# One DVE cost counted as 1.9 instead of 1.2, and a reordered start and last step, in a kernel bound by TensorE

## Chip, cores and metric

One core of one Trainium2 chip. The metric is the device time of the kernel in microseconds (us). Engines are named as in the profile: PE (TensorE matmuls), DVE (VectorE), ACT (ScalarE), POOL (GpSimd), SP (SyncE, which here only issues DMAs). "L685" is line 685 of the kernel in question; the same statement has different line numbers before and after the change, so the text says each time which statement is meant.

## The reference, cut to what matters

```python
# x: [32, 512, 512] float32; adj: 512 x 512 of 0 and 1, about 0.8% ones
h = relu(layernorm(x))                                   # layer 0
q, k, v = h @ Wq, h @ Wk, h @ Wv                         # 8 heads of 64
attn = softmax(q k^T / 8 + (1 - adj) * -1e9)
x = x + (attn v) @ Wo + bo

h = relu(layernorm(x))                                   # layer 1
hw = h @ W
e = leaky_relu(s1[i] + s2[j]) * adj                      # s1 = hw @ a1, s2 = hw @ a2
x = x + elu(softmax(e) @ hw + beta * hw)
```

## The kernel before

The kernel walks over the 32 graphs in overlapping steps: step b computes the attention of graph b while it does Wo for graph b-1 and layer 1 for graph b-2. Each of the 512x512x512 products with a weight (Q, K, V, Wo, and W of layer 1) is done as 7 products of 256-blocks instead of 8; such a product is 7 "pieces" of 1.73 us on PE, with additions on DVE and POOL around them. A head pair is a "unit" (four in a step, numbered 0 to 3, so the third is j == 2, called unit 2): 4 groups of scores, exponentials on ACT, sums of them on DVE (`total`), the product with the values, and a division (`finish`: a reciprocal on DVE, a DMA round trip that spreads it, a multiply on POOL).

In the traces of the kernel before, DVE runs its instructions in the order in which the program issues them: the lines of all 4207, in the order of their starts, are those of the built program. Where a DVE instruction goes is decided by a reckoned clock, when the program is built:

```python
def pe(us):                                   # called after each piece of PE work
    clock["pe"] += us
    till = clock["pe"] + (1.0 if at_ends[0] else 0.4)
    while True:
        ...
        fits = [(by, i) for i, (_, t, cost, _, by) in enumerate(spare)
                if max(clock["dve"], t) + cost <= till]
        ...
            run_spare(min(fits)[1])           # earliest "by" first
        ...                                   # nothing fits: go on with PE

def later(key, wait, by, cost, fn):           # puts an item into the list of spare DVE work
    now = max(clock["dve"], clock["pe"])
    spare.append((key, now + wait, cost, fn, now + by))
```

So the cost given to `later` is not a statement about the chip. It is a number that decides what stands in front of what in DVE's queue.

```python
# scores: the sums of exponentials of unit j (k = 1, 2, 3)
later("es", 2.2 if k < T - 1 and b > 1 else 1.2, gap(b, j) - 6.0 + k, 1.2, lambda: total(k, e))

# finish: the division
def divide():
    nc.vector.reciprocal(rq, pd)                       # 1.75 us
    then("rd", spread)                                 # DMA round trip, then a multiply on POOL
later("rd", 0.0, gap(b, (j + 1) % NP) - 4.0, 1.7, divide)

# out_proj: what empties the banks of the Wo product
def add(i, k, p):
    for r, p_ in parts(k, i, p):
        nc.vector.scalar_tensor_tensor(r, p_, 1.0 / VS, r, op0=ALU.mult, op1=ALU.add)
def more(q_):                                          # shares of the second piece, on POOL
    for i in (1, 0):
        for r, q in parts(1, i, q_):
            nc.gpsimd.tensor_tensor(r, r, q, op=ALU.add)

# diagonal of layer 1: row sums by matmul, then the diagonal blocks
product(nc, pd[:, t, :], mixed(st["as"])[:, t, :], ones[:, :HD], ...)
for k in range(T):
    nc.vector.scalar_tensor_tensor(d, ident, bd[:, k : k + 1], d, op0=ALU.mult, op1=ALU.add)

# row_constants: 16 dots of W with a, once, in the start
later("wa", 8.0, 60.0, 0.5, lambda g=g, c=c, o=o, ar=ar: dot(g, c, o, ar))

# order of the parts of a step; digits are units, "." their denominators
order = {
    0: "0.V1.NH2c.3wK.Q", 1: "0.VUrR1.W2.NH3K.Q", B - 1: "0.VDU1.rRGX2.W3.t", B: "0yrR.zUWDngY",
    B + 1: "DgJY",
}.get(b, "0.VDU1.rgY2.RMNH3.KQ")     # V, K, Q: products; M, W: Wo; D: diagonal; g, G: gather; Y: product with W
```

## Time and profile before

| | before |
|---|---|
| time, median of 3 (lowest, highest) | 3651.6 us (3647.19, 3654.03) |
| profiled span | 3650.6 us |
| PE idle in the whole span | 124 us |
| of these between 200 and 3490 us (steps 2 to 30) | 66.6 us |
| mean granted PE clock | 0.992 |

PE is busy for 97% of the span and nothing else comes near. Such a profile is read from its gaps: which gap comes back in every step, who ended it, and what stood in front of that releaser in its own queue. The lines are in the prediction below. In a list of waits, "PE qz_w L53 <- DVE x L685: 42.7, 28, 2.6" means: before writing the bank qz_w, PE stood idle 42.7 us in all, 28 times, at most 2.6 us, and the last thing that it waited for was the DVE instruction of line 685. In a timeline a line is start, duration, engine, line, operation, and in brackets the idle time before it and who ended that.

### The profile page before, as it was taken

The numbers are of one execution on the slowest core, as the hardware profiler recorded it, in microseconds if no ns is written. First come the engines' busy times: TensorE is split into PE (matmuls) and PEld (weight loads), VectorE is DVE, ScalarE is ACT, GpSimd is POOL, SyncE is SP. The second block draws the span as 40 slices with busy tenths as digits, with TensorE's granted clock in tenths as the row PEclk, the third lists the DMA queues.
The fourth block names the chain that finished last, engine by engine and source line by source line (L and its number), as shares of the span: only waits on it lengthen the run. The fifth ranks groups of instructions, "written<-read, shape, count | busy, mean of one in ns | idle before, by whom it ended". The sixth has DMA issues, their size and how long they took to land. (4 is left out here: it accounts for less than half of the span.)

```text
span 3650.6 us, 64127 instructions
## 1 busy us (share of the span) xinstructions
PE 3526.5 (97%) x26358; PEld 1884.4 (52%) x26358; DVE 2757.1 (76%) x4207; ACT 1459.3 (40%) x2310; POOL 1320.0 (36%) x1090
## 2 busy tenths in 40 slices
PE   9899999999999999999999999999999999999986
PEld 5455554555555555545555555555455555455543
DVE  6778777778777787777787777877777877777774
ACT  3344434334443444343344434443434444343432
POOL 5333343333333333433333333334333333423341
PEclk9999999999999999999999999999999999999997
DMA  4011111101111011111011110111110111111110
GB/s 134 18 33 44 47 47 44 36 27 47 47 47 36 30 45 47 47 44 36 27 47 47 47 38 28 44 47 47 44 36 27 47 47 47 47 32 31 41 38 27
DMA packets 109548, 155.02 MB, mean 42 GB/s; under 512 B 16513, under 2 KB 54913, under 8 KB 109249
## 3 DMA queue, kind: packets, MB, share of 16 engines
q1 hardware_dynamic: 106640, 148.49, 12.9%
q8 instruction: 209, 3.42, 0.4%
q10 hardware_dynamic: 2400, 2.10, 0.2%
q14 instruction: 91, 0.74, 0.1%
q0 software_dynamic: 208, 0.27, 0.0%
HBM read 116.66 MB, written 34.15 MB: 41 GB/s over the span
## 5 line engine op out<-in xcount | busy, mean ns | idle before, releaser
L585 ACT ACTIVATE e<-e 128x1024 f32<-128x1024 f32 x512 | 541.3, 1057 | 263.4 <-DVE e L570 227.3
L570 DVE SCALAR_TENSOR_TENSOR e<-maskT,ps 128x1024 f32<-128x1024 uint8 x384 | 455.7, 1214 | 115.6 <-PE ps L558 115.3
L558 PE MATMUL ps<-qT,kT 64*128 64x512 f32 x2048 | 490.0, 608 | 27.5 <-DVE dmax L798 18.1
L645 POOL TENSOR_TENSOR oT<-oT,rd 128x512 f32<-128x512 f32 x128 | 167.6, 1310 | 864.1 <-DMA rd<-rd 710.6
L608 PE MATMUL po<-e,v 128*64 128x512 f32 x2048 | 463.2, 594 | 0.0
L53 PE MATMUL pg<-at,hn 128*64 128x512 f32 x2048 | 451.6, 599 | 4.2 <-DVE dmax L798 2.1
L558 PEld LDWEIGHTS ps<-qT,kT 64*128 64x128 f32 x2048 | 184.4, 186 | 329.8 <-issue 155.2
L582 DVE TENSOR_TENSOR es<-es,e 128x1024 f32<-128x1024 f32 x254 | 342.3, 1348 | 15.2 <-ACT e L585 0.7
L501 POOL TENSOR_TENSOR qT<-qT,edge 128x256 f32<-128x256 f32 x128 | 85.4, 689 | 658.9 <-DVE qT L497 658.8
L53 PEld LDWEIGHTS pg<-at,hn 128*64 128x64 f32 x2048 | 146.4, 138 | 293.9 <-issue 284.7
L359 DVE TENSOR_SCALAR x<-x,mv,rs 128x512 f32<-128x512 f32 x128 | 104.5, 858 | 226.9 <-POOL rs L334 226.7
L608 PEld LDWEIGHTS po<-e,v 128*64 128x64 f32 x2048 | 141.9, 137 | 235.5 <-issue 223.6
L834 POOL TENSOR_TENSOR y<-y,x 128x512 f32<-128x512 f32 x124 | 159.2, 1288 | 191.2 <-DVE y L826 188.1
L635 DVE RECIPROCAL rd<-pd 128x256 f32<-128x256 f32 x128 | 223.9, 1749 | 3.1 <-POOL oT L645 3.1
L664 POOL TENSOR_TENSOR x<-x,c_row 128x512 f32<-128x512 f32 x124 | 165.2, 1352 | 100.8 <-DMA x<-in_x_dram 100.8
L766 ACT ACTIVATE at<-at 128x512 f32<-128x512 f32 x128 | 80.7, 630 | 278.2 <-DVE at L762 277.0
L53 PE MATMUL qz_y<-w,vT 128*64 128x256 f32 x1520 | 181.3, 381 | 4.1 <-DVE yq L847 4.1
L582 DVE TENSOR_TENSOR es<-e,e 128x1024 f32<-128x1024 f32 x127 | 172.4, 1357 | 0.8 <-PE pd L626 0.8
L824 DVE TENSOR_SCALAR y<-y 128x512 f32<-128x512 f32 x128 | 55.3, 432 | 155.5 <-ACT y L821 155.1
L812 ACT COPY gT<-pg 128x512 f32<-128x512 f32 x128 | 74.9, 585 | 243.9 <-PE pg L53 243.9
L53 PE MATMUL qz_w<-wo,uT 128*64 128x256 f32 x1040 | 127.6, 388 | 46.3 <-DVE x L685 42.7
L739 DVE CUSTOM_DVE_ANT_0 scr<-hn,wa_r 128x512 f32<-128x512 f32 x256 | 163.6, 700 | 0.1
(223 smaller groups left out, 6395.6 us busy)
## 6 DMA issues: line engine op xcount, KB each, us to landing
x<-in_x_dram SPq DMA_DIRECT2D x128, 256.0 KB, 4.0
rd<-rd SPq DMA_DIRECT2D x256, 128.0 KB, 2.9
out_dram<-y SPq DMA_DIRECT2D x128, 256.0 KB, 4.0
x<-in_x_dram SPq DMA_DIRECT2D x63, 512.0 KB
s<-row_s SPq DMA_DIRECT2D x32, 256.0 KB, 3.8
rd<-rd ACTq DMA_DIRECT2D x128, 4.0 KB
adj<-in_adj_dram SPq DMA_DIRECT2D x4, 256.0 KB, 6.4
wk<-in_L_gnn_Wk_dram ACTq DMA_DIRECT2D x3, 256.0 KB
```

Of the source, the lines that this page charges most:

```text
L53: nc.tensor.matmul(out[s : s + HD], lhsT[:, s : s + HD], rhs, start=start, stop=stop, skip_group_check=onto)
L359: nc.vector.tensor_scalar(xs[t], xs[t], mv[:, t, 0:1], rstd[:, t : t + 1], op0=ALU.subtract, op1=ALU.mult)
L558: nc.tensor.matmul(ps[s], st["kT"][j][rows, ts(k, P)], st["qT"][j][rows, :], start=True, stop=True)
L570: nc.vector.scalar_tensor_tensor(e, maskT[:, k, :].unsqueeze(1).to_broadcast([P, 2, N]), NEG, p, op0=ALU.mult, op1=ALU.add)
L582: (nc.gpsimd if early else nc.vector).tensor_tensor(es, one, e, op=ALU.add)
L585: nc.scalar.activation(e, e, AF.Exp)
L608: nc.tensor.matmul(po[s * HD : (s + 1) * HD, :], v[k // 2][:, k % 2, (2 * j + s) * HD : (2 * j + s + 1) * HD], e[k][:, s, :], start=k == 0 ...
L635: nc.vector.reciprocal(rq, pd)
L645: then("rd", lambda: nc.gpsimd.tensor_tensor(o, o, rd, op=ALU.mult), 6.0)
L664: eng.tensor_tensor(r[:, t, :], r[:, t, :], c_row, op=ALU.add)
L739: nc.vector.tensor_tensor_reduce(scr, st["hn"][t], r, 1.0, 0.0, op0=ALU.mult, op1=ALU.add, accum_out=st["s12"][:, g, t : t + 1],)
L834: (nc.vector if b == B - 2 else nc.gpsimd).tensor_tensor(yu, yu, x_[:, :, ts(i, H)], op=ALU.add)
```

## The change

It is meant to rearrange the last step (logits sooner, diagonals inside the Wo product and inside the final product, no DMA trip in the last division), to move the 16 dots of the start, and, in every step from 2 on, to count the sums of exponentials of the third unit (j == 2) as 1.9 us instead of 1.2. Cut to its core:

```diff
-                    later("wa", 8.0, 60.0, 0.5, ...dot...)
+                    later("wa", 40.0, 75.0, 0.5, ...dot...)
...
-                    "es", 2.2 if k < T - 1 and b > 1 else 1.2, gap(b, j) - 6.0 + k, 1.2, lambda: total(k, e)
+                    "es", 2.2 if k < T - 1 and b > 1 else 1.2, gap(b, j) - 6.0 + k, 1.9 if j == 2 and b > 1 else 1.2,
+                    lambda: total(k, e)
...
+        if (b, j) == (B - 1, NP - 1):
+            return finish_last(b, j, st)
...
-        later("rd", 0.0, gap(b, (j + 1) % NP) - 4.0, 1.7, divide)
+        later("rd", 0.0, gap(b, (j + 1) % NP) - 4.0 if (b, j) != (0, NP - 1) else 0.0, 1.7, divide)
+    def finish_last(b, j, st):      # 2 matmuls spread the denominators; no DMA
...
+        def divide(k):
+            nc.vector.reciprocal(pd[:, ts(k, H)], pd[:, ts(k, H)])
+            if k:
+                nc.vector.tensor_tensor(o, o, pd, op=ALU.mult)
...
-        eng = nc.vector if b == B - 1 else nc.gpsimd         # residual rows
-                eng.tensor_tensor(r[:, t, :], r[:, t, :], c_row, op=ALU.add)
+                nc.gpsimd.tensor_tensor(r[:, t, :], r[:, t, :], c_row, op=ALU.add)
...
-            for i in (1, 0):
+            def share(i):
                 for r, q in parts(1, i, q_):
                     nc.gpsimd.tensor_tensor(r, r, q, op=ALU.add)
+            share(1)
+            st["share"] = lambda: share(0)
...
             fourth(b - 1, "uT", prev["oT"])      # combination t4, on POOL
+            prev["share"]()                       # second share now behind it
             run(pieces)
...
-            0: "0.V1.NH2c.3wK.Q", 1: "0.VUrR1.W2.NH3K.Q", B - 1: "0.VDU1.rRGX2.W3.t", B: "0yrR.zUWDngY",
-            B + 1: "DgJY",
+            0: "0.V1.NH2c.3wK.Q", 1: "0.VUrR1.W2.NH3K.Q", B - 1: "0.VDU1.rRGX2.W3.ft",
+            B: "0p.qmURzviDlngPES", B + 1: "gJY",
```

Cut away: the helpers behind the new letters. Of those, "i" is six of the seven Wo pieces, with step 30's totals forced in; "l" is the last piece, behind the diagonal; "P", "E" and "S" are the same for the final product.

More of the change, by code (lines that the diff above doesn't have):

```diff
@@ L323, in row_constants @@
                 for o in range(2):
-                    later("wa", 8.0, 60.0, 0.5, lambda g=g, c=c, o=o, ar=ar: dot(g, c, o, ar))
+                    later("wa", 40.0, 75.0, 0.5, lambda g=g, c=c, o=o, ar=ar: dot(g, c, o, ar))
     def stats(src, name, mv):
@@ L648, in finish @@
         release()
-        later("rd", 0.0, gap(b, (j + 1) % NP) - 4.0, 1.7, divide)
+        later("rd", 0.0, gap(b, (j + 1) % NP) - 4.0 if (b, j) != (0, NP - 1) else 0.0, 1.7, divide)
+    def finish_last(b, j, st):
+        pd = psum.tile([P, N], F32, name=f"pd_{b}_{j}", tag="pd")
+        for s in range(2):
+            nc.tensor.matmul(
+                pd[s * HD : (s + 1) * HD, :], ones[:, :HD], st["es"][j][:, s, :], start=True, stop=True
+            )
+        pe(0.95)
+        o = st["o"][j // 2][:, j % 2, :]
+        def divide(k):
+            nc.vector.reciprocal(pd[:, ts(k, H)], pd[:, ts(k, H)])
+            if k:
+                nc.vector.tensor_tensor(o, o, pd, op=ALU.mult)
+        finished.add((b, j))
+        st["largest"] = lambda: nc.scalar.activation(
+            pd, pd, AF.Copy, accum_out=rsum[:, b, j : j + 1]
+        )
+        for k in range(2):
+            later("rd", 0.0, 0.0, 1.7 + 0.7 * k, lambda k=k: divide(k))
     def residual(b, st, i, tag="x1", bufs=3):
@@ L894, in G, with first_y, more_y @@
                 gather(b - 2, c, old)
+        def first_y(g):
+            states[g]["pieces"] = final(g, states[g])
+            next(states[g]["pieces"])
         def y_(g):
+            first_y(g)
+            more_y(g)
+        def more_y(g):
             st = states[g]
-            st["pieces"] = final(g, st)
-            for _ in range(3):
+            for _ in range(2):
                 next(st["pieces"])
@@ L911, in Y, with most_of_y @@
             z_(b - 2)
+        def most_of_y():
+            y_(b - 2)
+            run_all(("at", b - 1))
+            for _ in range(3):
+                next(old["pieces"])
         def X():
@@ L928, in W, with most_of_w @@
         def W():
+            most_of_w()
+            run(prev["pieces"])
+        def most_of_w():
             need("wa")
             fourth(b - 1, "uT", prev["oT"])
-            run(out_proj(b - 1, prev))
+            prev["pieces"] = out_proj(b - 1, prev)
+            for k in range(6):
+                next(prev["pieces"])
+                if k == 1:
+                    prev["share"]()
+                elif k == 2 and b == B:
+                    run_all(("at", b - 2))
         def H_():
@@ L952, in M @@
             fourth(b - 1, "uT", prev["oT"])
+            prev["share"]()
             run(pieces)
@@ L960, in step @@
             "y": lambda: y_(b - 3), "z": lambda: z_(b - 3), "X": X, "M": M, "g": G1,
-            "K": K, "U": U, "H": H_, "r": lambda: residual(b - 1, prev, 0, *(("e", 4) if b == B else ())),
+            "K": K, "U": U, "H": H_, "r": lambda: residual(b - 1, prev, 0),
             "t": T1, "n": lambda: run_all(("hn", b - 1)), "J": judge,
@@ L964, in step @@
             "Q": lambda: run(proj_q(b + 1, nxt)),
+            "p": lambda: first_y(b - 3), "q": lambda: more_y(b - 3), "v": lambda: prev["largest"](),
+            "m": lambda: run_all(("hn", b - 2)),
+            "i": most_of_w, "l": lambda: run(prev["pieces"]),
+            "P": most_of_y, "E": lambda: diagonal(b - 1, prev), "S": lambda: z_(b - 2),
+            "f": lambda: residual(b, cur, 0, "x", 4),
             "c": lambda: value_row(ao, bvr), "w": row_constants,
```

## The prediction

> **What bounds the kernel now.** I read the page first, then who waited for whom on PE, then PE's timeline over the whole span with its gaps, and last the timelines of DVE and POOL around the gaps that come back.
>
> ```profile
> span 3650.6 us, 64127 instructions
> PE 3526.5 (97%) x26358; PEld 1884.4 (52%) x26358; DVE 2757.1 (76%) x4207; ACT 1459.3 (40%) x2310; POOL 1320.0 (36%) x1090
> ```
>
> PE is the bound: 97% busy, DVE next with 76%. Nothing in the change takes matmuls away, so all it can win is the 124 us (3650.6 - 3526.5) in which PE stands still, and the time in which PE runs at a lower granted clock because it stood still. So the question is where those 124 us are:
>
> ```profile
> PE qz_w L53 <- DVE x L685: 42.7, 28, 2.6
> PE pe L53 <- DVE as L773: 20.4, 2, 13.0
> PE ps L558 <- DVE dmax L798: 18.1, 24, 1.3
> ...
> PE qz_w L53 <- POOL uT L399: 2.4, 2, 1.3
> ```
>
> Columns: total us, times, longest. Two of these come back every step (28 and 24 times in 32 steps of about 111.4 us), one sits in the last two steps (twice, up to 13 us). The first is the last piece of the Wo product. One step of it, PE and then DVE:
>
> ```profile
> 1739.54 1.95 PE L53 MATMUL qz_w<-wo,uT 128*64 128x256 f32 x16 [1.17 <-DVE x L685]
> ...
> 1735.26 1.74 DVE L635 RECIPROCAL rd<-pd 128x256 f32<-128x256 f32 x1
> 1736.92 0.62 DVE L685 SCALAR_TENSOR_TENSOR x<-x_w,x 128x512 f32<-128x512 f32 x1
> 1737.47 1.32 DVE L582 TENSOR_TENSOR es<-es,e 128x1024 f32<-128x1024 f32 x1
> 1738.71 0.68 DVE L685 SCALAR_TENSOR_TENSOR x<-qz_w,x 128x512 f32<-128x512 f32 x1
> ```
>
> PE may not write that bank again before the second L685 has read it, and ahead of that L685 in DVE's queue stand a reciprocal (1.74) and the last sum of exponentials (1.32) of unit 2. The second recurring wait is behind the diagonal; PE, DVE, POOL:
>
> ```profile
> 2135.74 3.27 PE L558 MATMUL ps<-qT,kT 64*128 64x512 f32 x12 [0.70 <-DVE dmax L798]
> ...
> 2130.84 4.62 DVE L792 SCALAR_TENSOR_TENSOR at<-ident,bd,at 128x128 f32<-128x128 f32 x4
> ...
> 2131.15 1.28 POOL L645 TENSOR_TENSOR oT<-oT,rd 128x512 f32<-128x512 f32 x1 [20.44 <-DMA rd<-rd]
> ...
> 3564.53 1.51 DVE L792 SCALAR_TENSOR_TENSOR at<-ident,bd,at 128x128 f32<-128x128 f32 x4
> ```
>
> The four small L792 take 4.62 us beside POOL's multiply and the three combinations after it, and 1.51 us where POOL is idle (last line, in the tail). The start and the tail:
>
> ```profile
> 128.69 2.08 PE L558 MATMUL ps<-qT,kT 64*128 64x512 f32 x4 [3.64 <-DVE e L570]
> ...
> 157.99 2.91 PE L53 MATMUL qz_w<-wo,oT 128*64 128x256 f32 x16 [2.80 <-POOL oT L379]
> ...
> 3563.00 1.23 PE L53 MATMUL pe<-ones,as 128*64 128x64 f32 x16 [7.41 <-DVE as L773]
> ...
> 3608.76 1.23 PE L53 MATMUL pe<-ones,as 128*64 128x64 f32 x16 [12.96 <-DVE as L773]
> ...
> 3612.07 16.14 PE L53 MATMUL pg<-at,hn 128*64 128x512 f32 x64 [2.08 <-DVE dmax L800]
> ```
>
> A gather (x64) takes 13.95 us in the middle of the kernel and 16.14 us here: PE runs at the low clock for a while after the long wait.
>
> [...] the mean granted clock is 0.51 in 7 us around the 3.64 us wait at 128 us, and 0.66 in the 5 us from the end of two of the three waits of 2.5 us (622 and 1626 us; 1.00 at 959); it stays 1.00 after the waits of 1.5. [...] 4.62 against 1.51 us above; L582 takes 1.2 us alone and 2.1 beside POOL. [...]
>
> **The change part by part.**
>
> *1. Third unit's sums counted as 1.9 instead of 1.2.* No instruction is added. The kernel keeps a reckoned clock for PE and DVE, and puts a spare DVE item into the queue when (DVE clock + cost) is within 0.4 of the PE clock. I followed that rule by hand through a middle step; with 1.2 it gives DVE's order in the trace. Zero is the start of unit 2's scores. PE's clock after Wo pieces 1 to 7 is 5.76, 7.49, 9.22, 10.95, 12.68, 14.41, 16.14.
> Before: piece 2 takes two normalisations (6.95), piece 3 sums 1 and 2 (9.35), piece 4 the reciprocal (9.35 + 1.7 = 11.05, limit 11.35), then L685, then piece 5 sum 3 (11.8 + 1.2 = 13.0, limit 13.08): the order that costs the wait.
> After: piece 3 has room only for sum 1 (8.85), piece 4 for sum 2 (10.75); in piece 5 neither the reciprocal (11.7 + 1.7 = 13.4) nor sum 3 (13.6) fits under 13.08, nor in piece 6. They go behind piece 7. L685 then runs as soon as piece 5 is done, about 1.7 us before PE needs its bank. That removes the waits of steps 2 to 30: 42.7 - 0.8 (step 1) + 2.4 (the combination t4, which now also goes before the second share on POOL, 1.3 to 1.7 us sooner) = **-44 us**, and two spells of low clock after waits of 2.54 (groups of 3.06 and 3.54 us instead of 1.95): **-3**.
>
> *2. Its consequence at the diagonal.* By the same rule the backlog of about 3 us moves the dots, the logits and the totals later through K, Q and V; the last total then stands right before the diagonal, and the reciprocal of unit 3, so far in the fourth piece of V, goes behind it. So POOL's multiply, which follows it by a DMA round trip (5.2 us from reciprocal's end to L645), no longer lies beside L792: 1.5 instead of 4 to 5 us, and scores need not wait. What that wait costs is more than its 0.70: from 2133.90 to the next group at 2138.93 are 5.03 us, without the wait 3.64, so 1.4; 24 such and 5 of about 0.7 (2245 us) make 37. The order is delicate, so I count **-30**. Against it: the last total ends by my count 12.05 us after V's start and the diagonal wants it at 12.13; a semaphore's latency of 0.1 to 0.2 gives **+3** over the 28 steps.
>
> *3. Start.* The 16 dots (L309) become ready at +40 instead of +8, so the five us of them at 122.4 to 127.4, directly ahead of the scores' L570, go away: 3.64 of wait and 3.0 of low clock (2.08 + 1.08 + 3.52 against 1.07 + 0.64 + 1.95). The reciprocal of (0,3), now due at once, ran at 144.8 and can run near 130; POOL's combinations, which PE waited 2.80 + 1.7 of low clock for, come some 14 us sooner. Sum 11; other spare items take the place of the dots, so **-10**.
>
> *4. Tail, from 3514 on.* The last division loses its DMA trip: two reciprocals of 1.75 on DVE and a multiply (about 0.7) instead of one reciprocal and 128 KB twice. Added for PE: two matmuls, 0.9. Residual rows move from DVE (3.57 us) to POOL. Laid out by the trace's durations: the denominator must wait for the former one's copy (3522.7): PE loses 3. The dots of step 30, 1.6 us each beside POOL and ended at 3547.4, end near 3533, so its logits are done about 3550 behind the elu's. The diagonal goes into Wo before its last piece, the gather starts at about 3554.5 instead of 3566.3 and keeps the full clock: end 3568.5 against 3583.0, **14** won. Step 31's logits: statistics from 3555, dots to 3564, row back at 3569.5 (before 3578.9); its totals by 3577.5 beside the last product of step 30. Three elu's of DVE (9.1 us as at 3591 to 3600) stand before the diagonal's own 2 us, so the last gather starts at about 3588.5 instead of 3612.1: 23 won; the rest (38.5 us) stays. I take **-21**.
>
> Sum: -10 - 44 - 3 - 30 + 3 - 21 = -105; 3651.6 - 105 = about **3547 us**.
>
> **Rivals.** (a) *Only the Wo wait goes.* The totals come too late at the diagonal, or the reciprocal does not move as reckoned, so that a wait on L773 takes the place of that on L798. For it: the margin of 0.1 us. Then -75, 3577, at the edge of 2%. (b) *DVE's backlog turns into new waits in K, Q or unit 3*, because 0.7 x 3 us is reckoned each step and other items come in front of evictions. For: DVE stands at 76%, 77 in the middle. Against: real items are shorter than their reckoned cost (dots 0.62 against 0.8, logits 1.39 against 1.5). With 1 us per step it makes 3580 to 3590. (c) *The tail gains nothing*: the long waits there are on chains (dots, row through DRAM, exponentials), and reordering moves the wait; then 3565. (d) All of parts 1 and 2, and no new wait: 3535.
>
> **Range and chances.** Part 1 is nearly sure (44 of 47), parts 3 and 4 are 31 give or take 10, part 2 is 0 to 37. The range reaches from all of it (3525) to part 2 missing with a weaker tail (3582). Two per cent is 73 us, 3578.6: 86% faster, 13% within, 1% slower.
>
> **What will show it.** Right, if the list of PE's waits has no more L685 line in the middle, if L792 in the middle takes 1.5 us for four and L798 is gone, if steps are 108.5 to 109 us long, if nothing waits at 128 us, and if the last gather starts about 24 us nearer to the end of step 31's scores. Wrong, if L773 or es shows as PE's releaser some 28 times, or if PE's waits on kT, qT or e appear in K, Q or unit 3.

## The result, and the profile after

| | median us | lowest to highest | runs |
|---|---|---|---|
| before | 3652.82 | 3647.19 to 3656.22 | 4 |
| after | 3560.49 | 3559.8 to 3561.33 | 4 |

The ratio is 0.9749, 95% interval 0.9732 to 0.9766: 2.5% faster. Here and below a ratio is the mean time of one kernel's runs over that of the other's of the same rounds, so it is not quite the ratio of the medians quoted. The page of the kernel after:

```profile
span 3559.0 us, 64141 instructions
PE 3506.1 (99%) x26353; PEld 1885.4 (53%) x26354; DVE 2727.3 (77%) x4207; ACT 1452.9 (41%) x2310; POOL 1396.6 (39%) x1095
```

PE does the same work in 20 us less busy time and is idle 53 us instead of 124. Busy time falls in part because PE runs less at the low clock (mean granted clock 0.994 instead of 0.992), and in part because a group of matmuls that a wait splits takes longer: in the prediction's example 5.03 us instead of 3.64 for a listed wait of 0.70, at a granted clock of 1.00. Who waits on PE now, after:

```profile
PE ps L558 <- DVE e L570: 11.6, 6, 8.5
PE qz_w L53 <- DVE y L853: 5.8, 1, 5.8
PE pg L53 <- DVE dmax L827: 5.5, 1, 5.5
```

The two lines that came back 28 and 24 times are gone, and so are both waits on the totals (`as`). What is left are single waits in the start and the tail. Between 200 and 3400 us PE is busy for 3198.4 of 3200 us.

**Where the 92 us come from.** I cut the two timelines at the same piece of work, the first piece of a Wo product, in step 2 and in step 31. Before, then after:

```profile
277.57 1.95 PE L53 MATMUL x_w<-wo,oT 128*64 128x256 f32 x16
...
3494.47 1.95 PE L53 MATMUL x_w<-wo,oT 128*64 128x256 f32 x16
```

```profile
280.08 1.95 PE L53 MATMUL x_w<-wo,oT 128*64 128x256 f32 x16
...
3412.79 1.95 PE L53 MATMUL x_w<-wo,oT 128*64 128x256 f32 x16
```

| stretch | before | after | difference | predicted |
|---|---|---|---|---|
| start, to the Wo product of step 2 | 277.6 | 280.1 | +2.5 | -10 |
| middle, 29 steps | 3216.9 (110.93 each) | 3132.7 (108.03 each) | -84.2 | -74 (-44 - 3 - 30 + 3) |
| tail, from the Wo product of step 31 | 156.1 | 146.2 | -9.9 | -21 |
| sum | 3650.6 | 3559.0 | -91.6 | -105 |

So over nine tenths of the gain is in the middle, where the only changes are the cost of 1.9 and the place of one share on POOL. The rearranged last step, which is most of the diff, gives a tenth.

**The Wo product in the middle, after** (DVE, then PE; compare the step at 1739 us in the prediction):

```profile
1696.70 0.68 DVE L709 SCALAR_TENSOR_TENSOR x<-x_w,x 128x512 f32<-128x512 f32 x1
1698.11 0.69 DVE L709 SCALAR_TENSOR_TENSOR x<-qz_w,x 128x512 f32<-128x512 f32 x1 [0.73 <-POOL uT L399]
...
1702.00 1.75 DVE L638 RECIPROCAL rd<-pd 128x256 f32<-128x256 f32 x1
...
1699.45 1.90 PE L53 MATMUL qz_w<-wo,uT 128*64 128x256 f32 x16
```

L709 is the former L685. The one that frees the bank qz_w ends at 1698.80; PE comes for it at 1699.45 and has no bracket, so no wait. The reciprocal, and after it the third sum, now stand behind it.

**The diagonal in the middle, after** (DVE):

```profile
1648.15 1.55 DVE L819 SCALAR_TENSOR_TENSOR at<-ident,bd,at 128x128 f32<-128x128 f32 x4
...
1650.00 1.76 DVE L638 RECIPROCAL rd<-pd 128x256 f32<-128x256 f32 x1
```

The four small instructions take 1.55 us instead of 4.62, as the reciprocal comes behind them and POOL's multiply, which hangs on it, starts only at 1657.09. All 128 of them, single durations (shortest, median, longest, in ns), before and after:

```profile
L792 DVE SCALAR_TENSOR_TENSOR at<-ident,bd,at x128: 436/1457/1657, 235.8 to 3611.3; 128x128 f32<-128x128 f32 x128
```

```profile
L819 DVE SCALAR_TENSOR_TENSOR at<-ident,bd,at x128: 437/455/1628, 237.6 to 3520.3; 128x128 f32<-128x128 f32 x128
```

**The start, after.** PE, DVE and POOL:

```profile
152.50 2.08 PE L558 MATMUL ps<-qT,kT 64*128 64x512 f32 x4 [8.48 <-DVE e L570]
165.11 2.83 PE L53 MATMUL qz_w<-wo,uT 128*64 128x256 f32 x16 [2.35 <-ACT qz_w L464]
...
136.74 0.42 DVE L309 CUSTOM_DVE_ANT_0 scr<-w,a 128x256 f32<-128x256 f32 x1
137.08 1.49 DVE L309 CUSTOM_DVE_ANT_0 scr<-a_w,a 128x256 f32<-128x256 f32 x1
...
151.24 1.21 DVE L570 SCALAR_TENSOR_TENSOR e<-maskT,ps 128x1024 f32<-128x1024 uint8 x1
...
139.67 5.68 POOL L688 TENSOR_TENSOR x<-x,c_row 128x512 f32<-128x512 f32 x4
```

The waits of 3.64 at 128 us and of 2.80 at 158 us are gone, as predicted. In their place stands one of 8.48 us: the dots (L309) did not go away but stand before a later L570, and most of them take 1.47 to 1.49 us instead of 0.42. The first, at 136.74, still takes 0.42: POOL was between two instructions, of which one ended at 136.80 and the next started at 136.88. From 135.53 to 151.03 POOL is busy, with no break over 0.1 us.

**The tail, after** (DVE, then POOL):

```profile
3447.19 1.22 DVE L748 SCALAR_TENSOR_TENSOR nb<-mv,rs 128x2 f32<-128x2 f32 x1 [3.71 <-POOL rs L334]
...
3459.32 2.79 DVE L853 SCALAR_TENSOR_TENSOR y<-yq,rd,y 128x256 f32<-128x256 f32 x2
...
3467.16 1.64 DVE L789 SCALAR_TENSOR_TENSOR at<-at 128x512 f32<-128x512 f32 x1
...
3445.21 1.27 POOL L648 TENSOR_TENSOR oT<-oT,rd 128x512 f32<-128x512 f32 x1 [12.73 <-DMA rd<-rd]
3446.45 0.71 POOL L334 TENSOR_TENSOR rs<-rs,mhalf 128x2 f32<-128x2 f32 x1
```

The two waits on the totals (7.41 and 12.96 us) have become 1.8 and 2.78, but new ones of 5.75 and 5.52 have come. The lines show what makes the first gather late: the same instructions of DVE take 2 to 3 times as long where POOL now works beside them (L853 took 0.88 for two before, L789 0.69), and DVE stands idle 3.71 us for a root on POOL that is queued behind a multiply that waits for a DMA. The wait of 5.52, before the last gather, is of another kind: three elu's stand before the last diagonal in DVE's queue, as the prediction had laid it out, and they take their usual time.

### The profile page after: what moved, and what is told of

It reads as the page before. It is cut to its first block, busy times and chain, and to the rows that moved or that the text cites.

```text
span 3559.0 us, 64141 instructions
## 1 busy us (share of the span) xinstructions
PE 3506.1 (99%) x26353; PEld 1885.4 (53%) x26354; DVE 2727.3 (77%) x4207; ACT 1452.9 (41%) x2310; POOL 1396.6 (39%) x1095
## 4 chain that ended last, share of the span: by engine, by line
PE 94%; DVE 4%; DMA 1%; POOL 0%; issue 0%; ACT 0%; SPq 0%; POOLq 0%; ACTq 0%; DVEq 0%
PE ps L558 12%; PE pg L53 12%; PE po L609 12%; PE qz_k L53 5%; PE qz_q L53 5%; PE qz_v L53 5%; PE qz_w L53 4%; PE qz_y L53 4%; PE x_k L53 3%; PE x_v L53 3%; PE x_q L53 3%; PE y_k L53 3%; PE y_v L53 3%; PE y_q L53 3%; PE x_w L53 3%; PE y_w L53 3%
## 5 line engine op out<-in xcount | busy, mean ns | idle before, releaser
L570 DVE SCALAR_TENSOR_TENSOR e<-maskT,ps 128x1024 f32<-128x1024 uint8 x384 | 456.4, 1216 | 85.4 <-PE ps L558 85.2
L558 PE MATMUL ps<-qT,kT 64*128 64x512 f32 x2048 | 478.1, 604 | 12.7 <-DVE e L570 11.6
L582 DVE TENSOR_TENSOR es<-es,e 128x1024 f32<-128x1024 f32 x254 | 381.8, 1503 | 11.0 <-DVE es L582 0.5
L861 POOL TENSOR_TENSOR y<-y,x 128x512 f32<-128x512 f32 (+1 forms) x126 | 159.5, 1271 | 186.8 <-DVE y L853 183.7
L688 POOL TENSOR_TENSOR x<-x,c_row 128x512 f32<-128x512 f32 x128 | 193.3, 1530 | 98.9 <-DMA x<-in_x_dram 98.9
L359 DVE TENSOR_SCALAR x<-x,mv,rs 128x512 f32<-128x512 f32 x128 | 103.5, 851 | 158.7 <-POOL rs L334 158.5
L582 DVE TENSOR_TENSOR es<-e,e 128x1024 f32<-128x1024 f32 x127 | 189.7, 1494 | 0.9 <-PE pd L629 0.8
L565 DVE SCALAR_TENSOR_TENSOR e<-maskT,ps 128x512 f32<-128x512 uint8 x256 | 163.6, 680 | 0.0
```

The costliest lines, as they stand in the source:

```text
L558: nc.tensor.matmul(ps[s], st["kT"][j][rows, ts(k, P)], st["qT"][j][rows, :], start=True, stop=True)
L565: nc.vector.scalar_tensor_tensor(e[:, s, :], maskT[:, k, :], NEG, ps[s], op0=ALU.mult, op1=ALU.add)
L570: nc.vector.scalar_tensor_tensor(e, maskT[:, k, :].unsqueeze(1).to_broadcast([P, 2, N]), NEG, p, op0=ALU.mult, op1=ALU.add)
L582: (nc.gpsimd if early else nc.vector).tensor_tensor(es, one, e, op=ALU.add)
L688: nc.gpsimd.tensor_tensor(r[:, t, :], r[:, t, :], c_row, op=ALU.add)
L861: (nc.vector if b == B - 2 else nc.gpsimd).tensor_tensor(yu, yu, x_[:, :, ts(i, H)], op=ALU.add)
```

## The experiments

Twelve kernels ran in three calls, each on another chip; each gave the right result. The kernel before ran along in each call, with medians of 3653.22, 3646.93 and 3651.8 us. The kernel after itself was not run again. So where an experiment is compared with it to within some us, I go by the place of the same work in the traces and by the other kernels of the same call. The quoted expectations name theories by letters; those that the verdicts rest on are: A, the gain of the middle comes from DVE's order alone, as predicted; B, it needs the new place of t4 and of the share on POOL; C, a gain in proportion to the cost added; E, the start lost by the dots beside POOL; F, it lost for another reason; H, in the tail PE waits for the sum of DVE's dots, division and elu's, whatever their order (for e12 the same letter also forecast a gain from moving the dots behind the elu's).

| label | base, and what differs | median us | ratio to before [95%] |
|---|---|---|---|
| e1_cost_alone | before, cost 1.9 | 3573.69 | 0.9775 [0.9745, 0.9804] |
| e2_cost_1p3 | before, cost 1.3 | 3618.14 | 0.9902 [0.9872, 0.9933] |
| e3_rest_alone | after, cost 1.2 | 3642.69 | 0.9975 [0.9963, 0.9988] |
| e4_recip_in_v | after, reciprocal of unit 3 in V | 3678.55 | 1.0061 [1.0031, 1.0091] |
| e5_recip_late | before, that reciprocal behind the diagonal | 3620.43 | 0.9899 [0.9868, 0.9931] |
| e6_dots_early | after, dots as before | 3552.30 | 0.9739 [0.9725, 0.9752] |
| e7_w1_late | after, combinations of W later | 3560.28 | 0.9760 [0.9747, 0.9774] |
| e8_tail_cost | after, cost 1.2 in step 31 | 3557.01 | 0.9750 [0.9737, 0.9764] |
| e9_dots_early_w1_late | e6 and e7 | 3549.72 | 0.9730 [0.9716, 0.9743] |
| e10_both_ends | e9 and e8 | 3548.85 | 0.9719 [0.9706, 0.9733] |
| e11_recip_before_dots | e10, last reciprocal sooner | 3548.86 | 0.9721 [0.9707, 0.9735] |
| e12_dots_after_elu | e10, dots behind the elu's | 3548.28 | 0.9717 [0.9703, 0.9730] |

### One number alone, and all but that number

e1_cost_alone is the kernel before with one line changed, e3_rest_alone the kernel after with that line undone:

```diff
-   ... gap(b, j) - 6.0 + k, 1.2, lambda: total(k, e)
+   ... gap(b, j) - 6.0 + k, 1.9 if j == 2 and b > 1 else 1.2, lambda: total(k, e)
```

> The kernel before with nothing of the change but the cost of 1.9 for the third unit's sums. Theory A (that one number reorders DVE's queue and takes away both recurring waits): the middle wins its whole 84 us, the start and the tail stay as before: 3565 to 3572, no wait of PE on L685 and none on L798 in the middle. Rival B (the new place of t4 and of the second share on POOL is needed for the wait in Wo): the waits behind Wo stay in part, with POOL L399 as releaser; 3600 or more.

> The kernel after with the cost back at 1.2: start, tail and the new place of t4 and of the second share, without the number. Theory A: both recurring waits are back in the middle (about 42 us on L709, which is L685 of before, and 18 us on L825), only the t4 waits (2.4 us) go; the start loses 2.3, the tail wins 12 to 14: about 3638 to 3642. Rival B (the new place of t4 and the share takes a good part of the Wo waits by itself): 3620 or less.

e1 alone gives 79.5 us (its time is 1.7 above the expected range), with the middle at 3134.9 us (82.0 less than before; the kernel after: 84.2 less). PE's waits start with the old one of the tail and have none of the middle:

```profile
PE pe L53 <- DVE as L773: 20.5, 2, 13.0
```

e3 gives 9.1 us, and the two waits of the middle are back:

```profile
PE qz_w L53 <- DVE x L709: 47.5, 29, 2.6
PE ps L558 <- DVE dmax L825: 17.3, 22, 1.2
```

79.5 + 9.1 = 88.6 of the 92. A is right and B falls: t4 and the share on POOL, which e1 leaves where they were, are worth at most the 2 us between the two middles, and in e3, which has them, the middle (3219.4 us) is no shorter than before. e3 was 0.7 us above its range. e1's start is 1.8 us longer than before. Its tail, at 158.5 us, is 2.4 longer: the cost of 1.9 also applies in step 31, where it does harm (e8 below).

### Order or size: a cost of 1.3

```diff
+   ... 1.3 if j == 2 and b > 1 else 1.2, lambda: total(k, e)
```

> The kernel before with a cost of 1.3 instead of 1.9. By the kernel's rule 1.3 is enough to push the last sum behind the second L685, but leaves the reciprocal of unit 3 in V, ahead of the diagonal. Theory A: the Wo waits go (44 to 47 us), the 24 waits on L798 stay: 3603 to 3610. Rival C (what counts is how much backlog is reckoned, so 0.1 wins a seventh of what 0.7 wins): about 3640.

By hand, 1.3 pushes sum 3 out of piece 5 but leaves the reciprocal in piece 4. So it should move one of the two items in front of L685, and it did (DVE, then PE):

```profile
1602.95 1.75 DVE L635 RECIPROCAL rd<-pd 128x256 f32<-128x256 f32 x1
...
1605.16 0.67 DVE L685 SCALAR_TENSOR_TENSOR x<-qz_w,x 128x512 f32<-128x512 f32 x1
...
1605.98 1.95 PE L53 MATMUL qz_w<-wo,uT 128*64 128x256 f32 x16 [0.26 <-DVE x L685]
```

The wait on L685 fell from 42.7 to 14.3 us, the middle by 39.6. Of the 24 waits on L798, 18 stayed, so some of the 39.6 comes from the diagonal. The time is 8 us above the expected range, since I had taken the wait for gone: with the reciprocal still in front, PE waits about 0.55 us in most steps. C, which would put a seventh of the added cost at a seventh of the gain (3640), falls. As far as two costs can show it, the gain goes in jumps, one for each item that changes its place.

### The diagonal: the reciprocal in front of it or behind it

e5_recip_late takes the kernel before and moves only the reciprocal of unit 3 behind the diagonal (in steps 1 to 30; the expected text says 31). e4_recip_in_v takes the kernel after and puts it back in front:

```diff
 # e5, on before
+        held_back = j == NP - 1 and 0 < b < B - 1
-        later("rd", 0.0, gap(b, (j + 1) % NP) - 4.0, 1.7, divide)
+        later("rd", 9.5 if held_back else 0.0, gap(b, (j + 1) % NP) - 4.0, 1.7, divide)
 # e4, on after
+        if j == NP - 1 and b:
+            later("rd", 3.0, -100.0, 1.7, divide)
+        else: (as it was)
```

> The kernel before, with only the reciprocal of unit 3 held back until behind the diagonal (steps 1 to 31), cost 1.2. Theory A: the waits on L798 go (37 us by the gaps in PE, 18 us by the list of waits), the Wo waits stay with 42: 3612 to 3622. Rival D: no change, 3650. If only the listed 18 us count: 3634.

> The kernel after, with the reciprocal of unit 3 put back into the fourth piece of V, in front of the diagonal (steps 1 to 31). Theory A: POOL's multiply and combinations lie beside L819 again, four of them take 4 to 5 us instead of 1.5, some 24 waits on the diagonal's dmax come back with 1.4 us each: 3585 to 3598. Rival D (those waits went because of the later logits or because PE came at another moment): within 5 us of 3560.

e5 takes 28.8 us from the middle (3188.1). The wait behind the diagonal is gone, the median of the four small instructions is 459 ns, and the waits of the Wo product are all still there, some 4 us longer in all (44.3 + 4.5 against 42.7 + 2.4).

With those 4 us added back, 33: close to the 37 that the prediction worked out and then cut to 30. So the second part of the gain is the reciprocal's place, and it can be had without the cost of 1.9. It is not the 1.75 us of the reciprocal itself: before the diagonal DVE stands idle for 1.93 us, waiting for PE, in nearly every step of the kernel before and of e5 alike. What differs is the four small instructions.

e4 went in the expected direction and far past the expected size (3585 to 3598): 3678.6, slower than the kernel before. The instructions at the diagonal are long again:

```profile
L822 DVE SCALAR_TENSOR_TENSOR at<-ident,bd,at x128: 439/1454/1607, 238.2 to 3638.1; 128x128 f32<-128x128 f32 x128
```

But that is only part of it. V has room for the reciprocal or for the totals, not for both, so the totals ran over V's end and a sum of exponentials came in front of the next unit's scores:

```profile
PE ps L558 <- DVE dmax L828: 39.1, 29, 1.6
PE ps L558 <- DVE e L570: 37.6, 33, 8.5
PE pe L53 <- DVE as L803: 31.2, 29, 3.1
```

The third of these lines is the wait that rival (a) of the prediction had named. It exists, though not in the kernel after. e4 is thus no clean measure of the diagonal; e5 is.

### The start

```diff
 # e6, on after
-                    later("wa", 40.0, 75.0, 0.5, ...dot...)
+                    later("wa", 8.0, 60.0, 0.5, ...dot...)
 # e7, on after: the combinations of W (POOL) behind the Wo product of step 1
-                if g == 1:
-                    combine(nc.gpsimd, w1, aw)
             most_of_w()
             run(prev["pieces"])
+            if b == 1:
+                combine(nc.gpsimd, w1, aw)
```

> The kernel after, with the dots of a and W (L309) ready at +8 again as before, everything else as after. The start of after lost 2.3 us by the beginning of step 1's Wo (155.5 against 153.2) where 10 were forecast to be won. Theory E (the dots only moved to another place where POOL works beside them and PE waits behind them): the wait of 8.5 us on e at 152 goes, the one of 3.6 at about 128 comes back with its 3 us of low clock; the earlier reciprocal of (0,3) is left as the gain: step 1's Wo begins near 148 to 151, time 3554 to 3558. Rival F (the loss at the start comes from the reciprocal of (0,3), now due at once): the start stays at 155 or later, 3560 or more.

> The kernel after, with POOL's five combinations of W1 (L281 to L287) issued only after step 1's Wo. Theory E says that the dots take 1.47 us instead of 0.42 [...]: the last 5 of the long dots lie beside these combinations, so the wait of 8.5 us at 152 becomes about 4 us, time 3554 to 3558. The rest of the dots lie beside POOL's L378 to L688 and stays slow. Rival (the dots are slow for another reason, such as their own row of a or their buffers): no change.

> The kernel after, with both: dots ready at +8 and POOL's combinations of W1 only after step 1's Wo. Theory E: dots in K and Q with POOL idle take 0.42 us each, so neither the wait at 128 nor the one at 152 is left: step 1's Wo begins near 144 to 147, time 3549 to 3553. Rival F: no better than the dots early alone.

e6 has the old wait at 128 us (3.61) back and not the one of 8.48; the Wo product of step 2 starts at 272.3 us instead of 280.1. That settles that the new place of the dots is what the start lost by (E): a loss of 8 us, not a gain, and F falls. The time came out 1.7 us below the expected range. What else was changed wins 5 by that point (277.6 before, 272.3 here); of that only the sooner reciprocal of the first graph was aimed at the start, and no run has it alone.

e7 keeps the late dots and takes a part of POOL's work from beside them. The mechanism shows: the dots from 147.32 us on take 0.42 us each (POOL's instruction before them ended at 146.92) and the wait becomes 5.57. But the time stays (3560.28, expected 3554 to 3558): PE now waits 5.06 us at 177.59, for a DVE that stands idle for a root on POOL:

```profile
172.43 1.26 POOL L646 TENSOR_TENSOR oT<-oT,rd 128x512 f32<-128x512 f32 x1 [9.52 <-DMA rd<-rd]
173.65 0.71 POOL L332 TENSOR_TENSOR rs<-rs,mhalf 128x2 f32<-128x2 f32 x1
174.33 1.26 POOL L281 TENSOR_TENSOR w<-a_w,w 128x512 f32<-128x512 f32 x1
```

The moved combinations (L281) come behind the root (L332), so they do not hold it up. The multiply in front of it does, and that waits for the division's DMA. The reciprocal had ended at 159.10, but SP issued its way back from DRAM only at 167.67: from 156.00 on it stood for 10.7 us for the second row of the dots, which goes through DRAM on the same queue. So the late dots hold up the start in a second way. In the kernel after the order on SP is the same: the row leaves at 157.86, SP waits 10.5 us for it, and the division's DMA is issued at 169.22, though its reciprocal had ended at 163.29; in e6, with the dots early, SP issues the division's DMA at 160.67 and the multiply runs at 164.46.

e9, with both, has dots of 0.42 us (two take longer, 0.72 and 1.00) and no wait at 128 or 152, and lies in its range.

It comes out 2.6 us under e6. Part of what it wins by 146.6 us (the Wo product of step 1) it gives back in a wait of 3.29 inside that product.

### The tail

```diff
 # e8, on after (and in e10 to e12)
-   1.9 if j == 2 and b > 1 else 1.2
+   1.9 if j == 2 and 1 < b < B - 1 else 1.2
 # e11 and e12, on e10: order of step 32
-   "0p.qmURzviDlngPES"
+   "0p.qUmRzviDlngPES"      # e11: the last reciprocal ahead of step 30's dots
+   "0p.qURzmviDlngPES"      # e12: those dots behind the elu's
```

> The kernel after, with the cost of 1.9 not used in the last step (31). In the tail of after DVE stood idle for 3.7 us for POOL's L334, which stood behind POOL's multiply and its DMA, since the statistics of two rows had been pushed behind the scores of unit 3. Theory G: without the 1.9 there, the statistics come before unit 3 again, the 3.7 us go and the first gather of the tail begins 3 to 5 us sooner: 3554 to 3557. Rival (the tail is held by the order of dots, second reciprocal and elu's alone): within 1 us of 3560.

> The kernel after, with dots ready at +8, the combinations of W1 after step 1's Wo, and no 1.9 in the last step. If the repairs of the start (10.7 us) and of the tail (3.5 us) are independent: 3545 to 3548. If one undoes the other: 3549 to 3553.

> The same as the run with both ends repaired, but in the tail the last division is forced before the dots of step 30 instead of behind them. Theory H (in the tail PE waits for DVE's sum of dots, division and elu's, in whatever order, since all stand in front of the elu's that free the banks): within 2 us of the run with both ends. Rival: the division's result (the second half of the last head pair, for the combinations of Wo) is what is late, then 3 to 5 us better.

> The same as the run with both ends repaired, but in the tail the dots of step 30 come behind the rest of the product of step 29. Theory H: the elu's no longer stand behind 5.6 us of dots, so the waits of 2 us on yq and 4 us on y go; the logits have some 8 us to spare behind the elu's (their row lands that much before they run), so 3 to 6 us better than the run with both ends, 3540 to 3544. Rival: the dots, the row through DRAM and the logits are the longer chain, and the diagonal in Wo waits for the totals by what the dots come later: the same or worse by up to 5 us.

e8 takes away the idle 3.7 us of DVE in the tail (142.0 us instead of 146.2) and is 3.3 us under e7, whose tail is that of the kernel after. e10 puts the better ends together. Its 3548.85 lies between the range for independent repairs (up to 3548) and that for repairs that undo each other (from 3549); in its trace both hold (start 270.7, tail 142.0). e11 left the time as it was, as expected. e12 missed: 3 to 6 us less than e10 were expected, and it lies within the others' spread. In both the waits only moved: 1.82, 5.73 and 0.60 us in e10 are 4.91, 0.42 and 3.53 in e11 and 4.34, 0.17 and 4.20 in e12. From the end of the last sums of exponentials to the end of the diagonal, DVE is busy for 37.35 of 40.99 us in e10, 37.46 of 41.26 in e11 and 35.98 of 39.66 in e12. This fits H as it was put for e11: the sum of DVE's work sets the end of this stretch, whatever its order. What fell is the gain that e12 drew from it.

e10 to e12 cannot be told apart. They are the fastest group, about 12 us (0.3%) under the kernel after and 2.8% under the kernel before.

## Why the prediction was right or wrong

The time was 3560.5 against 3547 predicted, within the range; the gain 92 us instead of 105. By its steps:

**1. Third unit's sums (predicted -44 - 3): right.** The order that I had worked out by hand from the reckoned clock is the one in the trace, the L685 line is gone, and e1, e2 and e3 show that the one number does it. No gain here rests on the number's being truer: the sums take about 1.2 us alone and 2.1 beside POOL, and 1.3 already changes half of the order.

**2. The diagonal (predicted -30 + 3): mechanism right, size too cautious.** The wait that was worked out as 37 went entirely. The discount to 30 was for an order that I called delicate; it held in all steps. The +3 for totals that come too late, worked out with 0.1 to 0.2 us from DVE's end to PE's start (0.15 in the step quoted at 1739.54 us), did not come: PE's waits after have no line for it. 44 + 3 + 37 = 84, and 84.2 is what the middle gained; such an agreement to 0.2 us is in part luck: e5 gives 33 for this part by itself, which leaves 51 and not 47 for the first, so the split is known to some 5 us only. e5 shows the mechanism by itself, and e4 shows that rival (a)'s wait lies close by. Rival (b), a wait in K, Q or unit 3 in place of the old ones, did not come: between 285 and 3400 us PE waits twice, for 0.5 us each.

**3. The start (predicted -10, measured +2.5): wrong.** The step that failed is "the five us of them at 122.4 to 127.4 ... go away", with "other spare items take the place of the dots". The dots went to 136.7 to 151.2, again ahead of an L570, and there most cost three times as much, because POOL works beside them; through SP they also hold up the division of the next unit (see e7). That POOL was busy there is partly the work of the change: its sooner reciprocal brings POOL's multiply, combinations and residual rows forward (the multiply from 153.09 to 134.17). I had noted this as a gain only. With the dots at their old place the start does gain 5 us (e6); the dots turn that into a loss of 2.5.

**4. The tail (predicted -21, measured -9.9): mechanism right, terms mis-sized.** From the values of the last unit, the first gather was predicted at +40.0 us; it came at +50.3 (before: +51.9). The dots of step 30 were to end at +18.5 and ended at +20.0; in this stretch DVE stands idle for 3.7 us for the root on POOL, which the working did not have. From there to the gather it was to be 21.5 us and was 30.3: one elu took 4.1 us instead of 1.3 (+2.8), and the logits with their totals 11.8 instead of 7.8 (+4.0), both beside POOL; the other 2 us are not traced. From that gather to the last it was to be 34.0 us and was 38.1 (before: 45.8): the dots of step 31 ended after 11.7 us instead of 9.5, their row was back after 5.0 instead of 5.5, the logits with their totals took 10.3 instead of 8.0, three of them beside POOL. The three elu's and the diagonal took the 11 us that were counted. So the last gather came 9 us nearer to the end of step 31's scores and not 24, the one sign of the prediction in the tail, and it failed. e11 and e12 show that neither of two other orders helps.

Points 3 and 4 share one cause, though not all of either. I took durations of DVE instructions from rows in which POOL was idle, and used them in places to which the same change moves POOL's work, although the prediction itself had the 4.62 and the 1.51 us side by side.

What stays open: which terms of the tail could be had back. e8 shows it for the idle 3.7 us only.

## What to carry to other kernels

Where one engine is busy all the time, look for the instruction that ends its recurring wait, and then for what stands in front of that instruction in its own queue: one number that moves a reciprocal and a sum behind one such instruction, and another reciprocal behind the diagonal, was worth 80 us, about eight times as much as a rewritten last step. When a cost model decides the order, treat its numbers as switches, and work out by hand which items change places. Before moving DVE instructions like these dots, logits, sums and diagonals, which took 0.9 to 1.1 us longer each beside POOL, or anything that triggers POOL work, lay the two engines' timelines side by side at the new place: the durations at the old place do not carry over. Look at the DMA queue there too.

## What the traces show of DVE beside POOL, the clock and the reciprocal

- What a run of short DVE instructions pays beside POOL: each one that took longer there did so by somewhat less than one POOL instruction (1.27 to 1.5 us), whatever its own length: 0.42 to 1.48 (dots), 0.46 to 1.46 (diagonal), 0.69 to 1.64 (logits), 1.2 to 2.1 (sums), so by 0.9 to 1.1 us each. Many short instructions therefore suffered most: the four of a diagonal took 4.62 us instead of 1.51. A tensor_scalar in the elu's took longer too (0.43 to 1.30 us). The scores' L570 did not: in the kernel before its median is 1.21 us without POOL and 1.22 where POOL is busy for over half of it.
- After short waits of PE the granted clock was lower in some cases and not in others. After 2.35 us at 165 us in the kernel after, the mean granted clock of the next 5 us was 0.66, and the next two pieces took 2.83 and 2.75 us instead of 1.90. Before the change, two of three waits of 2.5 us had that effect (0.66 at 622 and 1626 us), one had not (1.00 at 959 us); nor had the wait of 2.24 us at 3440 us in the kernel after (1.00). A plan for a kernel like this one should count a part of such waits.
- A reciprocal took 1.75 us for 128x256 float32 from PSUM, against 0.68 for an addition of 128x512 elements: five times as long per element, which makes it the item to keep out of the way.
